# Attention and channel mixing of a transformer layer on one core: sums of the softmax weights in 32-column tiles spread by DMAs, one ring of score tiles, and fixed places for the side work

## The chip, the cores and the metric

The kernel runs on one core of a Trainium2 chip. A core has five engines that run their own instruction streams in order and wait for each other through semaphores: TensorE (PE in the profile; its weight loads are PEld), VectorE (DVE), ScalarE (ACT), GpSimd (POOL) and SyncE (SP), which here only issues DMAs. Matrix products are written to PSUM, eight banks of 512 fp32 columns in 128 partitions; everything else lives in SBUF. The metric is the device time of one execution in microseconds; lower is better. The kernel before takes 1331.07 us, the median of three runs from 1328.94 to 1338.77.

## The reference

Input x has 16 batches of 512 tokens with 128 channels. With xn the row-normalised x,

```python
xn = layernorm(x)                                   # (16, 512, 128)
# attention, 16 heads, key width 8, value width 64, causal
q, k, v = xn @ Wq, xn @ Wk, xn @ Wv
attn = softmax(where(causal, -inf, q k^T / sqrt(8)))
a = concat_heads(attn v) @ Wo
# channel mixing
xp = xn shifted down by one token, zeros first
xr, xk = mu_r*xn + (1-mu_r)*xp, mu_k*xn + (1-mu_k)*xp
f = sigmoid(xr @ W_r.T) * (relu(xk @ W_k.T)**2 @ W_v.T)
out = x + a + f
```

All of it is fp32.

## The kernel before, in words

The heads are taken in pairs, two pairs make a *group* (g, 0 to 3), and a batch has four groups. The causal blocks of a group (128 by 128 to 128 by 512) are packed into five *units* (`ROW_UNITS` for scores with rows in the partitions, `KEY_UNITS` for scores with keys in the partitions), so a batch has 20 units and the whole kernel 320. The program walks through *slots*, one for each unit (`slot_work(s)`, written out without loops on the chip). In slot s it does

- `row_scores` of unit s+8 (tile `sm`), of which VectorE takes the row maxima (`row_max`, tile `mx`); this finds the shift of the softmax ahead of time;
- `key_scores` of unit s (tile `sT`), with two extra rows of q that hold minus the row maximum in two parts, `weights` (Exp on ScalarE into tile `e`), the causal mask and the running sums `acc` on GpSimd;
- `weigh` of unit s-5, the product of the weights with v (tile `av`), and at the end of a pair `take_ctx`, which on VectorE multiplies `av` with the reciprocal sums (`recip`) into `ctx`. There is one `av` tile, so the next pair's first product waits for `take_ctx`.

Slots are named below by their number modulo 20 within a batch, and u is that number modulo 5. Around this come pieces of side work. `turn_stats` (once in a group) transposes the maxima on TensorE (`pm`), splits them on VectorE (`mh`, `ml`), and SP sends them with four DMAs into rows of q. `sum_weights` (twice in a group) sums weights over the keys with products by ones: tile `z`, 512 columns, two tiles of 64 array columns, one for each head; ScalarE makes the reciprocal by Ln and Exp(-x) into `recip`. `layernorm`, `transpose_xn`, `project_qk`, `spread_qk` and `project_v` prepare later batches: `spread_qk` is eight DMAs for q and eight for k in each batch, 128 KB each from DRAM into 8 partitions. `mix`, `ffn_r`, `ffn_k` and `ffn_out` are the channel mixing, `project_out` the product with Wo, `store` the result. The table built at the end of the kernel (`at(slot, ...)`) says in which slot each piece runs, always at the slot's end, ahead of `weigh`.

The engines are wrapped so that their instructions keep program order (`_InOrder`, line 57, which is why almost every profile line says L57); the order of the pieces is therefore written out by hand. Pools give tiles of one name a fixed number of buffers. PSUM is divided as follows: `ps_sm` three one-bank tiles, `ps_st` one two-bank tile, `ps_av` one bank, `ps_m` two banks (`m_tile`) that all side work shares: `xnTp`, `pq`, `pk`, `pv`, `pr`, `pkv`, `pm`, `z`, `po`, `yT`. `po` keeps one of the two for two slots, since `project_out` adds four pairs in it. All transfers of the steady state are issued by SP, in program order. In the built program they take eight completion semaphores in turn, and a transfer is issued only when the one before it on its semaphore, the eighth transfer back, has landed.

Of the kernel before, what the change touches and what calls it, by code (L numbers as in the profile page):

```python
# [15 lines left out]
P = 128  # L16
# [6 lines left out]
UNITS = 5  # L23
# [39 lines left out]
def attn_ffn_kernel(  # L63
# [26 lines left out]
    ctxp = ctx.enter_context(tc.tile_pool(name="ctxp", bufs=6))  # L90
# [4 lines left out]
    ps_sm = ctx.enter_context(tc.tile_pool(name="ps_sm", bufs=3, space=PSUM))  # L95
    ps_st = ctx.enter_context(tc.tile_pool(name="ps_st", bufs=1, space=PSUM))
    ps_av = ctx.enter_context(tc.tile_pool(name="ps_av", bufs=1, space=PSUM))
    ps_m = ctx.enter_context(tc.tile_pool(name="ps_m", bufs=2, space=PSUM))
# [94 lines left out]
    def layernorm(b):  # L193
        xt, st = xs[b], xs.pop((b, "st"))
        mv = small.tile([P, NB, 2], FP, tag="mv", name=f"mv_{b}")
        for c in range(NB):
            dve.bn_aggr(mv[:, c, :], st[:, c, :])
        ve = small.tile([P, NB], FP, tag="ve", name=f"ve_{b}")
        dve.tensor_scalar(ve, mv[:, :, 1], EPS, None, ALU.add)
        rstd = small.tile([P, NB], FP, tag="rstd", name=f"rstd_{b}")  # L200
        pool.tensor_tensor(rstd, ve, neg_half, ALU.pow)
        xn = one.tile([P, NB, D], FP, tag="xn", name=f"xn_{b}")
        for c in range(NB):
            dve.tensor_scalar(
                xn[:, c, :], xt[:, c, :], mv[:, c, 0:1], rstd[:, c : c + 1],
                ALU.subtract, ALU.mult,
            )
        xs[b, "n"] = xn
# [41 lines left out]
    def mix_prev(b, i):  # L250
        prev = one.tile([P, T], FP, tag="prev", name=f"prev_{b}_{i}")
        act.activation(prev, xnTs[b][:, 0:T], AF.Copy, scale=omm[:, i : i + 1])
        xmix[b, "prev"] = prev

    def mix(b, i):
        prev = xmix.pop((b, "prev"))
        xm = one.tile([P, T], FP, tag=f"xmix{i}", name=f"xmix_{b}_{i}")
        dve.scalar_tensor_tensor(
            xm, xnTs[b][:, 1 : T + 1], mus[:, i : i + 1], prev, ALU.mult, ALU.add
        )  # L260
        xmix[b, i] = xm


    def ffn_r(b):
        pr = m_tile(f"pr_{b}")
        product(pr, ffn_w[:, 0, :], xmix.pop((b, 0)))
        e = one.tile([P, T], FP, tag="e_sig", name=f"e_sig_{b}")
        act.activation(e, pr, AF.Abs)
        act.activation(e, e, AF.Exp, scale=-1.0)
        act.activation(e, e, AF.Ln, bias=1.0)  # L270
        s = one.tile([P, T], FP, tag="sig", name=f"sig_{b}")
        dve.scalar_tensor_tensor(s, pr, 0.0, e, ALU.min, ALU.subtract)
        ffns[b] = s

    def ffn_sig(b):
        act.activation(ffns[b], ffns[b], AF.Exp)
# [9 lines left out]
    def ffn_out(b):  # L286
        pk = m_tile(f"pkv_{b}")
        product(pk, ffn_w[:, 2, :], ffns.pop((b, "k")))
        f = one.tile([P, T], FP, tag="ffn", name=f"ffn_{b}")
        dve.tensor_tensor(f, pk, ffns[b], ALU.mult)  # L290
        ffns[b] = f
# [5 lines left out]
    def row_scores(n):  # L297
        b, g, u = place(n)
        q, k = qs[b % 2], ks[b % 2]
        for h in range(2):  # L300
            sms[n, h] = ps_sm.tile([P, 512], FP, tag="sm", name=f"sm_{n}_{h}")
        for pair, i, at_col in ROW_UNITS[u]:
            p = 2 * g + pair
            for h in range(2):
                s = slice(64 * h, 64 * h + RS)
                pe.matmul(
                    sms[n, h][:, at_col : at_col + (i + 1) * P],
                    q[s, p, i * P : (i + 1) * P], k[s, p, : (i + 1) * P],
                    start=True, stop=True,
                )  # L310

    def row_max(n, h):
        b, g, u = place(n)
        if u == 0 and h == 0:
            stats[b, g] = stat.tile([P, 2, 2, NB], FP, tag="mx", name=f"mx_{b}_{g}")
        sm = sms.pop((n, h))
        for pair, i, at_col in ROW_UNITS[u]:
            w = (i + 1) * P
            dve.tensor_tensor_reduce(
                out=sm[:, at_col : at_col + w], in0=sm[:, at_col : at_col + w],  # L320
                in1=row_mask[:, T - w : T],
                scale=1.0, scalar=LOWEST, op0=ALU.add, op1=ALU.max,
                accum_out=stats[b, g][:, h, pair, i : i + 1],
            )
# [89 lines left out]
    def sum_weights(q0, pair):  # L414

        e0, acc = es[q0 + 4 * pair], accs.pop((q0, pair))
        z = m_tile(f"z_{q0}_{pair}")
        for lo, hi, rhs in ((0, P, e0), (P, T, acc)):
            for h in range(2):
# [38 lines left out]
    def project_out(b, p):  # L458
        half = NPAIR // 2
        if p % half == 0:  # L460
            ffns[b, "po"] = m_tile(f"po_{b}_{p}")
        po = ffns[b, "po"]
        product(
            po, wo[:, p, :], ctxs.pop((b, p)), start=(p % half == 0), stop=(p % half == half - 1)
        )
# [16 lines left out]

    todo = {}

    def at(slot, f, *args):
        todo.setdefault(max(slot, -LEAD), []).append((f, args))

    for b in range(-2, B):
        s0 = b * PER_BATCH
        if 1 <= b + 2 < B:  # L490
            n = b + 2
            for c in range(NB):
                at(s0 + 5 + c, row_moments, n, c)
            at(s0 + 10, layernorm, n)
            at(s0 + 15, transpose_xn, n)
            at(s0 + 17, project_qk, n, False)
            at(s0 + 21, spread_qk, n, False)
            at(s0 + 23, project_qk, n, True)
# [12 lines left out]
        at(s0 + 1, ffn_r, b)  # L511
        at(s0 + 2, ffn_sig, b)
        at(s0 + 3, ffn_k, b)
        at(s0 + 4, ffn_out, b)
        for p, slot in enumerate((16, 16, 18, 18, 26, 26, 28, 28)):
            at(s0 + slot, project_out, b, p)
        at(s0 + 30, store, b)

    def slot_work(s):
# [3 lines left out]
        av_u = av % UNITS if av is not None else None  # L523
# [40 lines left out]
    take_ctx(N_UNITS - UNITS, 1)  # L564
    for s in sorted(todo):
        for f, args in todo[s]:
            f(*args)
# [31 lines left out]
```

## Time and profile before

| | us |
|---|---|
| median of 3 runs | 1331.07 (1328.94 to 1338.77) |
| profiled execution | 1328.98 |
| its span, first to last instruction | 1327.2 |
| TensorE busy | 1151.1 (87%) |
| VectorE / GpSimd / ScalarE busy | 811.8 / 733.2 / 641.2 |
| mean granted TensorE clock | 0.886 |
| first and last key scores start | 64.8 and 1309.9 |

Busy time is the union of an engine's instructions. The granted clock is the share of full speed at which TensorE was allowed to run; a matmul takes twice as long at 0.50. Durations below are means or medians of one instruction in this execution, so sums are made against its 1328.98 us, which is 2.1 us under the median.

### The profile page before, as it was taken

The page shows a single profiled execution, that of the slowest core. Times are in us where ns is not written, and L with a number is a line of the kernel's source. Part 1 is how long each engine was busy: PE and PEld are TensorE (multiplying, and loading weights), DVE is VectorE, ACT ScalarE, POOL GpSimd, SP SyncE. Part 2 cuts the span into 40 slices and gives each one's busy share as a digit, 9 for nine tenths or more (in the row PEclk, how much of TensorE's full clock was granted, in tenths as well). Part 3 has the DMA queues.
Part 4 walks back from the last instruction along what each step waited for, and adds up shares of the span by engine and source line. Part 5 has one row for each costly group of instructions (what it writes and reads, how often), then busy time and mean ns, then how long its engine had stood idle before and what let it go on. Part 6 is the DMA issues. An engine that isn't in the chain of part 4 may idle for free.

```text
span 1327.2 us, 19813 instructions
## 1 busy us (share of the span) xinstructions
PE 1151.1 (87%) x6659; PEld 492.3 (37%) x6659; DVE 811.8 (61%) x2659; ACT 641.2 (48%) x865; POOL 733.2 (55%) x964
## 2 busy tenths in 40 slices
PE   1779898898989988898898989888898898989898
PEld 0234343333434333343333334333343333434333
DVE  1575766656667556766646766665766656665741
ACT  0255555345554445555445554544545445455633
POOL 2065655556555555655546655555655655565645
PEclk9588998889889889989879988988988988998979
DMA  4440413205033130412304032231412304032000
GB/s 126 74 74 18 73 25 59 55 23 75 18 70 45 32 66 18 87 27 56 59 18 81 17 76 39 38 61 33 76 22 47 68 25 74 9 72 35 2 10 9
DMA packets 51509, 62.70 MB, mean 47 GB/s; under 512 B 6528, under 2 KB 26624, under 8 KB 51408
## 3 DMA queue, kind: packets, MB, share of 16 engines
q1 hardware_dynamic: 48768, 59.79, 24.5%
q10 hardware_dynamic: 2192, 1.38, 0.4%
q8 instruction: 53, 0.87, 0.3%
q0 software_dynamic: 448, 0.26, 0.2%
q14 instruction: 48, 0.39, 0.1%
HBM read 39.13 MB, written 20.97 MB: 45 GB/s over the span
## 4 chain that ended last, share of the span: by engine, by line
PE 62%; DVE 16%; DMA 8%; ACT 5%; POOL 5%; issue 3%; SPq 1%; DVEq 0%; POOLq 0%; ACTq 0%
PE av L57 17%; PE po L57 11%; PE z L57 9%; PE sm L57 8%; PE pv L57 6%; DVE sm L57 6%; PE sT L57 5%; DMA k<-k 4%; DVE xn L57 3%; PE pq L57 2%; ACT e_sig L57 2%; DVE xmix L57 2%; POOL acc L57 2%; DVE ctx L57 2%; ACT recip L57 2%
## 5 line engine op out<-in xcount | busy, mean ns | idle before, releaser
L57 DVE CUSTOM_DVE_ANT_0 sm<-sm,row_mask 128x384 f32<-128x384 f32 (+3 forms) x1024 | 495.3, 507 | 252.2 <-PE sm L57 237.5
L57 ACT ACTIVATE e<-sT 128x1024 f32<-128x1024 f32 x320 | 326.9, 1022 | 445.4 <-PE sT L57 440.3
L57 POOL TENSOR_SCALAR_AFFINE_SELECT e<-e 128x256 f32<-128x256 f32 (+1 forms) x448 | 197.6, 455 | 516.8 <-ACT e L57 513.3
L57 PE MATMUL av<-e,v 128*64 128x384 f32 (+3 forms) x2048 | 380.8, 474 | 7.6 <-DVE ctx L57 7.1
L57 POOL TENSOR_TENSOR acc<-acc,e 128x256 f32<-128x256 f32 (+1 forms) x256 | 255.8, 999 | 15.4
L57 POOL TENSOR_TENSOR acc<-e,e 128x768 f32<-128x768 f32 (+2 forms) x192 | 251.3, 1309 | 0.0
L57 PEld LDWEIGHTS av<-e,v 128*64 128x64 f32 x2048 | 148.3, 148 | 256.3 <-issue 202.3
L57 PE MATMUL sm<-k,q 33*128 33x384 f32 (+3 forms) x1024 | 184.2, 402 | 35.6 <-DVE mx L57 20.7
L57 PEld LDWEIGHTS sm<-k,q 33*128 33x128 f32 x1024 | 94.2, 206 | 226.0 <-issue 154.1
L57 PE MATMUL sT<-q,k 35*128 35x384 f32 (+3 forms) x1024 | 150.3, 344 | 5.9 <-DMA q<-ml 5.2
L57 PE MATMUL po<-ctx,wo 128*64 128x512 f32 x512 | 153.3, 729 | 0.0
L57 DVE DVE_READ_ACCUMULATOR2_ANT mx<- 128x1 f32 x1024 | 144.5, 141 | 0.0
L57 PE MATMUL pv<-wv,xnT 128*64 128x512 f32 x512 | 142.6, 658 | 0.0
L57 ACT ACTIVATE recip<-z 128x512 f32<-128x512 f32 x128 | 76.4, 597 | 129.9 <-PE z L57 129.9
L57 PE MATMUL z<-acc,ones 128*64 128x384 f32 x512 | 123.1, 557 | 0.0
L57 PE MATMUL z<-e,ones 128*64 128x128 f32 x512 | 58.9, 307 | 63.5 <-DVE ml L57 55.7
L57 DVE TENSOR_TENSOR ctx<-av,recip 128x512 f32<-128x512 f32 x128 | 88.3, 689 | 41.4 <-PE av L57 31.6
L57 PEld LDWEIGHTS sT<-q,k 35*128 35x128 f32 x1024 | 102.4, 205 | 14.9 <-issue 6.5
L57 ACT ACTIVATE v<-pv 128x512 f32<-128x512 f32 x128 | 76.5, 598 | 35.9 <-PE pv L57 35.9
L57 ACT ACTIVATE recip<-recip 128x512 f32<-128x512 f32 x128 | 80.7, 631 | 4.0
L57 PEld LDWEIGHTS z<-e,ones 128*64 128x64 f32 x512 | 27.7, 139 | 90.8 <-POOL e L57 60.8
L57 PEld LDWEIGHTS po<-ctx,wo 128*64 128x64 f32 x512 | 36.0, 157 | 59.1 <-issue 53.4
(63 smaller groups left out, 619.6 us busy)
## 6 DMA issues: line engine op xcount, KB each, us to landing
q<-q SPq DMA_DIRECT2D x120, 128.0 KB
k<-k SPq DMA_DIRECT2D x120, 128.0 KB
x<-in_L_attn_x_dram SPq DMA_DIRECT2D x16, 256.0 KB
q<-qh SPq DMA_DIRECT2D x16, 256.0 KB
q<-ql SPq DMA_DIRECT2D x16, 256.0 KB
k<-kh SPq DMA_DIRECT2D x16, 256.0 KB
k<-kl SPq DMA_DIRECT2D x16, 256.0 KB
out_dram<-o SPq DMA_DIRECT2D x16, 256.0 KB
```

What stands on the lines that cost most here:

```text
L57: return self._tc.keep_in_program_order(f(*args, **kwargs))
```

## The change

- PSUM: `sm` and `sT` come from one pool `ps_sc` of three two-bank tiles; `ps_m` has one bank instead of two.
- `sum_weights`: four tiles of 32 array columns; columns 0 to 255 and 256 to 511 of a head go to different partitions, so that `z` has 256 columns. Ln and Exp run on 256 columns into `half`; eight DMAs of 32 partitions by 1 KB (32 KB each), issued by SP, copy `half` into the full `recip`.
- Places: each piece of side work has a slot and one of three places in it: 0 after the scores, 1 after `sum_weights`, 2 after `weigh`. `sum_weights` runs at u = 4 and u = 1, `turn_stats` at the start of the slots with u = 2. `take_ctx` runs at the end of slots with u = 1 and u = 4, the former after the last product of the first pair, which is moved one slot earlier.
- `spread_qk`: 16 DMAs of 64 KB for q and 16 for k in a batch, in slots 1 to 4.
- `layernorm`: two passes of VectorE over 512 columns instead of four over 128. `mix`: both products on ScalarE and the sum on GpSimd. `ffn_r`: ScalarE copies `pr` to SBUF first. `project_out`: one group at a time, four sums on VectorE for a batch instead of two.

```diff
-    ps_sm = ctx.enter_context(tc.tile_pool(name="ps_sm", bufs=3, space=PSUM))
-    ps_st = ctx.enter_context(tc.tile_pool(name="ps_st", bufs=1, space=PSUM))
+    ps_sc = ctx.enter_context(tc.tile_pool(name="ps_sc", bufs=3, space=PSUM))
     ps_av = ctx.enter_context(tc.tile_pool(name="ps_av", bufs=1, space=PSUM))
-    ps_m = ctx.enter_context(tc.tile_pool(name="ps_m", bufs=2, space=PSUM))
+    ps_m = ctx.enter_context(tc.tile_pool(name="ps_m", bufs=1, space=PSUM))
...
-        for c in range(NB):
-            dve.tensor_scalar(
-                xn[:, c, :], xt[:, c, :], mv[:, c, 0:1], rstd[:, c : c + 1],
-                ALU.subtract, ALU.mult,
-            )
+        shape = [P, NB, D]
+        dve.tensor_tensor(xn, xt, mv[:, :, 0:1].to_broadcast(shape), ALU.subtract)
+        dve.tensor_tensor(xn, xn, rstd.unsqueeze(2).to_broadcast(shape), ALU.mult)
...
-    def mix_prev(b, i):
+    def mix(b, i):
+        xm = one.tile([P, T], FP, tag=f"xmix{i}", name=f"xmix_{b}_{i}")
         prev = one.tile([P, T], FP, tag="prev", name=f"prev_{b}_{i}")
+        act.activation(xm, xnTs[b][:, 1 : T + 1], AF.Copy, scale=mus[:, i : i + 1])
         act.activation(prev, xnTs[b][:, 0:T], AF.Copy, scale=omm[:, i : i + 1])
-        xmix[b, "prev"] = prev
-
-    def mix(b, i):
-        prev = xmix.pop((b, "prev"))
-        xm = one.tile([P, T], FP, tag=f"xmix{i}", name=f"xmix_{b}_{i}")
-        dve.scalar_tensor_tensor(
-            xm, xnTs[b][:, 1 : T + 1], mus[:, i : i + 1], prev, ALU.mult, ALU.add
-        )
+        pool.tensor_tensor(xm, xm, prev, ALU.add)
...
     def ffn_r(b):
         pr = m_tile(f"pr_{b}")
         product(pr, ffn_w[:, 0, :], xmix.pop((b, 0)))
+        s = one.tile([P, T], FP, tag="sig", name=f"sig_{b}")
+        act.activation(s, pr, AF.Copy)
         e = one.tile([P, T], FP, tag="e_sig", name=f"e_sig_{b}")
-        act.activation(e, pr, AF.Abs)
+        act.activation(e, s, AF.Abs)
         act.activation(e, e, AF.Exp, scale=-1.0)
         act.activation(e, e, AF.Ln, bias=1.0)
-        s = one.tile([P, T], FP, tag="sig", name=f"sig_{b}")
-        dve.scalar_tensor_tensor(s, pr, 0.0, e, ALU.min, ALU.subtract)
+        dve.scalar_tensor_tensor(s, s, 0.0, e, ALU.min, ALU.subtract)
+        act.activation(s, s, AF.Exp)
         ffns[b] = s
-
-    def ffn_sig(b):
-        act.activation(ffns[b], ffns[b], AF.Exp)
...
+        sm = sms[n] = ps_sc.tile([P, 2, 512], FP, tag="sc", name=f"sm_{n}")
...
-        st = sts[n] = ps_st.tile([P, 2, 512], FP, tag="sT", name=f"sT_{n}")
+        st = sts[n] = ps_sc.tile([P, 2, 512], FP, tag="sc", name=f"sT_{n}")
...
         e0, acc = es[q0 + 4 * pair], accs.pop((q0, pair))
         z = m_tile(f"z_{q0}_{pair}")
-        for lo, hi, rhs in ((0, P, e0), (P, T, acc)):
-            for h in range(2):
-                pe.matmul(
-                    z[64 * h : 64 * h + 64, lo:hi], ones, rhs[:, h, lo:hi],
-                    start=True, stop=True, skip_group_check=True,
-                )
+        for part in range(2):
+            for c in range(2):
+                if part and c:
+                    continue
+                lo, hi = ((0, P), (256, T))[c] if part == 0 else (P, 256)
+                for h in range(2):
+                    r = 64 * h + 32 * c
+                    pe.matmul(
+                        z[r : r + 32, lo - 256 * c : hi - 256 * c], ones[:, 0:32],
+                        (acc if lo else e0)[:, h, lo:hi],
+                        start=True, stop=True, skip_group_check=True,
+                    )
+        half = small.tile([P, 256], FP, tag="half", name=f"half_{q0}_{pair}")
+        act.activation(half, z[:, 0:256], AF.Ln)
+        act.activation(half, half, AF.Exp, scale=-1.0)
         r = small.tile([P, T], FP, tag="recip", name=f"recip_{q0}_{pair}")
-        act.activation(r, z, AF.Ln)
-        act.activation(r, r, AF.Exp, scale=-1.0)
+        for h in range(2):
+            for c in range(2):
+                for to in range(2):
+                    sp.dma_start(
+                        out=r[64 * h + 32 * to : 64 * h + 32 * to + 32, 256 * c : 256 * c + 256],
+                        in_=half[64 * h + 32 * c : 64 * h + 32 * c + 32],
+                    )
         recips[q0, pair] = r
...
-    def project_out(b, p):
-        half = NPAIR // 2
-        if p % half == 0:
-            ffns[b, "po"] = m_tile(f"po_{b}_{p}")
-        po = ffns[b, "po"]
-        product(
-            po, wo[:, p, :], ctxs.pop((b, p)), start=(p % half == 0), stop=(p % half == half - 1)
-        )
-        if p % half == half - 1:
-            y = one.tile([P, T], FP, tag=f"y{p // half}", name=f"y_{b}_{p}")
-            dve.tensor_tensor(y, po, ffns[b], ALU.add)
-            ffns[b] = y
+    def project_out(b, g):
+        po = m_tile(f"po_{b}_{g}")
+        for i in range(2):
+            product(po, wo[:, 2 * g + i, :], ctxs.pop((b, 2 * g + i)), start=i == 0, stop=i == 1)
+        dve.tensor_tensor(ffns[b], po, ffns[b], ALU.add)
...
-                at(s0 + 5 + c, row_moments, n, c)
-            at(s0 + 10, layernorm, n)
-            at(s0 + 15, transpose_xn, n)
-            at(s0 + 17, project_qk, n, False)
-            at(s0 + 21, spread_qk, n, False)
-            at(s0 + 23, project_qk, n, True)
-            at(s0 + 25, spread_qk, n, True)
+                at(s0 + 5 + c, 0, row_moments, n, c)
+            at(s0 + 10, 0, layernorm, n)
+            at(s0 + 12, 2, transpose_xn, n)
+            at(s0 + 15, 1, project_qk, n, False)
+            at(s0 + 17, 2, project_qk, n, True)
+            for i in range(2):
+                at(s0 + 21 + i, 0, spread_qk, n, False, slice(4 * i, 4 * i + 4))
+                at(s0 + 23 + i, 0, spread_qk, n, True, slice(4 * i, 4 * i + 4))
         if 0 <= b + 1 < B:
-            for n, slot in enumerate((9, 11, 11, 13, 13, 14, 19, 21)):
-                at(s0 + slot if b >= 0 else n - LEAD, project_v, b + 1, n)
+            places = ((5, 1), (8, 1), (9, 2), (10, 1), (13, 1), (14, 2), (18, 1), (19, 2))
+            for n, (slot, where) in enumerate(places):
+                if b >= 0:
+                    at(s0 + slot, where, project_v, b + 1, n)
+                else:
+                    at(n - LEAD, 1, project_v, b + 1, n)
         if b < 0:
             continue
         if b + 3 < B:
-            at(s0 + 12, load_x, b + 3)
-        at(s0 - 2, mix_prev, b, 0)
-        at(s0 - 1, mix, b, 0)
-        at(s0, mix_prev, b, 1)
-        at(s0 + 1, mix, b, 1)
-        at(s0 + 1, ffn_r, b)
-        at(s0 + 2, ffn_sig, b)
-        at(s0 + 3, ffn_k, b)
-        at(s0 + 4, ffn_out, b)
-        for p, slot in enumerate((16, 16, 18, 18, 26, 26, 28, 28)):
-            at(s0 + slot, project_out, b, p)
-        at(s0 + 30, store, b)
+            at(s0 + 12, 0, load_x, b + 3)
+        at(s0 - 3, 0, mix, b, 0)
+        at(s0 - 1, 0, mix, b, 1)
+        at(s0, 1, ffn_r, b)
+        at(s0 + 2, 2, ffn_k, b)
+        at(s0 + 4, 2, ffn_out, b)
+        for g in range(NQ):
+            at(s0 + 5 * g + 10, 2, project_out, b, g)
+        at(s0 + 27, 2, store, b)
...
     def slot_work(s):
         rows = s + LEAD if s + LEAD < N_UNITS else None
         keys = s if 0 <= s < N_UNITS else None
         av = s - LAG if 0 <= s - LAG < N_UNITS else None
-        av_u = av % UNITS if av is not None else None
+        u = s % UNITS
+        turned = s + LEAD - UNITS
+        if turned >= 0 and turned % UNITS == 0 and turned < N_UNITS:
+            b, g, _ = place(turned)
+            turn_stats(b, g)
         if rows is not None:
             row_scores(rows)
         if keys is not None:
@@ -528,27 +540,23 @@
             weights(keys)
             mask_weights(keys)
             add_weights(keys)
-        if av is not None and av_u == 0 and av >= UNITS:
-            take_ctx(av - UNITS, 1)
         if rows is not None:
-            row_max(rows, 0)
-        if av_u == 2:
-            weigh(av, only=0)
-            take_ctx(av - 2, 0)
-        if rows is not None:
-            row_max(rows, 1)
-        if 0 <= s + LEAD - UNITS < N_UNITS and (s + LEAD) % UNITS == 0:
-            b, g, _ = place(s + LEAD - UNITS)
-            turn_stats(b, g)
-        done = s - UNITS - (0 if s % UNITS == 0 else 2)
-        if s % UNITS in (0, 2) and 0 <= done < N_UNITS:
-            sum_weights(done, 0 if s % UNITS == 0 else 1)
-        for f, args in todo.pop(s, ()):
-            f(*args)
-        if av_u == 2:
-            weigh(av, only=1)
-        elif av is not None:
-            weigh(av)
+            row_max(rows)
+        run(s, 0)
+
+        if u == 4 and 0 <= s - 4 < N_UNITS:
+            sum_weights(s - 4, 0)
+        if u == 1 and 0 <= s - 6 < N_UNITS:
+            sum_weights(s - 6, 1)
+        run(s, 1)
+        if av is not None:
+            weigh(av, only=1 if u == 2 else None)
+            if u == 1:
+                weigh(av + 1, only=0)
+                take_ctx(av - 1, 0)
+            if u == 4:
+                take_ctx(av - 4, 1)
+        run(s, 2)
```

More of the change, by code (lines that the diff above doesn't have):

```diff
@@ L89, in attn_ffn_kernel @@
     ep = ctx.enter_context(tc.tile_pool(name="ep", bufs=LAG + 2))
-    ctxp = ctx.enter_context(tc.tile_pool(name="ctxp", bufs=6))
+    ctxp = ctx.enter_context(tc.tile_pool(name="ctxp", bufs=4))
     one = ctx.enter_context(tc.tile_pool(name="one", bufs=1))
@@ L288, in ffn_out @@
         product(pk, ffn_w[:, 2, :], ffns.pop((b, "k")))
-        f = one.tile([P, T], FP, tag="ffn", name=f"ffn_{b}")
+        f = small.tile([P, T], FP, tag="ffn", name=f"ffn_{b}")
         dve.tensor_tensor(f, pk, ffns[b], ALU.mult)
@@ L299, in row_scores @@
         q, k = qs[b % 2], ks[b % 2]
-        for h in range(2):
-            sms[n, h] = ps_sm.tile([P, 512], FP, tag="sm", name=f"sm_{n}_{h}")
+        sm = sms[n] = ps_sc.tile([P, 2, 512], FP, tag="sc", name=f"sm_{n}")
         for pair, i, at_col in ROW_UNITS[u]:
@@ L306, in row_scores @@
                 pe.matmul(
-                    sms[n, h][:, at_col : at_col + (i + 1) * P],
+                    sm[:, h, at_col : at_col + (i + 1) * P],
                     q[s, p, i * P : (i + 1) * P], k[s, p, : (i + 1) * P],
@@ L310, in row_scores, with row_max @@
                 )
-    def row_max(n, h):
+    def row_max(n):
         b, g, u = place(n)
-        if u == 0 and h == 0:
+        if u == 0:
             stats[b, g] = stat.tile([P, 2, 2, NB], FP, tag="mx", name=f"mx_{b}_{g}")
[L316 to L323, printed above, removed]
-            )
+        sm = sms.pop(n)
+        for h in range(2):
+            for pair, i, at_col in ROW_UNITS[u]:
+                w = (i + 1) * P
+                dve.tensor_tensor_reduce(
+                    out=sm[:, h, at_col : at_col + w], in0=sm[:, h, at_col : at_col + w],
+                    in1=row_mask[:, T - w : T],
+                    scale=1.0, scalar=LOWEST, op0=ALU.add, op1=ALU.max,
+                    accum_out=stats[b, g][:, h, pair, i : i + 1],
+                )
     def turn_stats(b, g):
@@ L417, in sum_weights @@
         z = m_tile(f"z_{q0}_{pair}")
-        for lo, hi, rhs in ((0, P, e0), (P, T, acc)):
-            for h in range(2):
-                pe.matmul(
-                    z[64 * h : 64 * h + 64, lo:hi], ones, rhs[:, h, lo:hi],
-                    start=True, stop=True, skip_group_check=True,
-                )
-        r = small.tile([P, T], FP, tag="recip", name=f"recip_{q0}_{pair}")
-        act.activation(r, z, AF.Ln)
-        act.activation(r, r, AF.Exp, scale=-1.0)
+        for part in range(2):
[13 more added lines that the diff above has]
+        act.activation(half, half, AF.Exp, scale=-1.0)
+        r = small.tile([P, T], FP, tag="recip", name=f"recip_{q0}_{pair}")
+        for h in range(2):
+            for c in range(2):
[3 more added lines that the diff above has]
+                        in_=half[64 * h + 32 * c : 64 * h + 32 * c + 32],
+                    )
         recips[q0, pair] = r
@@ L454, in take_ctx @@
         ctxs[b, 2 * g + pair] = c
-    def project_out(b, p):
-        half = NPAIR // 2
-        if p % half == 0:
-            ffns[b, "po"] = m_tile(f"po_{b}_{p}")
-        po = ffns[b, "po"]
-        product(
-            po, wo[:, p, :], ctxs.pop((b, p)), start=(p % half == 0), stop=(p % half == half - 1)
-        )
-        if p % half == half - 1:
-            y = one.tile([P, T], FP, tag=f"y{p // half}", name=f"y_{b}_{p}")
-            dve.tensor_tensor(y, po, ffns[b], ALU.add)
-            ffns[b] = y
+    def project_out(b, g):
[3 more added lines that the diff above has]
+        dve.tensor_tensor(ffns[b], po, ffns[b], ALU.add)
     def store(b):
@@ L483, in attn_ffn_kernel, with at @@
     todo = {}
-    def at(slot, f, *args):
-        todo.setdefault(max(slot, -LEAD), []).append((f, args))
+    def at(slot, where, f, *args):
+        if slot < -LEAD:
+            slot, where = -LEAD, 0
+        todo.setdefault((slot, where), []).append((f, args))
     for b in range(-2, B):
@@ L505, in attn_ffn_kernel, with run @@
         if b + 3 < B:
-            at(s0 + 12, load_x, b + 3)
-        at(s0 - 2, mix_prev, b, 0)
-        at(s0 - 1, mix, b, 0)
-        at(s0, mix_prev, b, 1)
-        at(s0 + 1, mix, b, 1)
-        at(s0 + 1, ffn_r, b)
-        at(s0 + 2, ffn_sig, b)
-        at(s0 + 3, ffn_k, b)
-        at(s0 + 4, ffn_out, b)
-        for p, slot in enumerate((16, 16, 18, 18, 26, 26, 28, 28)):
-            at(s0 + slot, project_out, b, p)
-        at(s0 + 30, store, b)
+            at(s0 + 12, 0, load_x, b + 3)
[7 more added lines that the diff above has]
+        at(s0 + 27, 2, store, b)
+    def run(s, where):
+        for f, args in todo.pop((s, where), ()):
+            f(*args)
     def slot_work(s):
@@ L563, in attn_ffn_kernel @@
         slot_work(s)
[L564 to L567, printed above, removed]
+    for s, where in sorted(todo):
+        run(s, where)
 _INS = [
```

## The prediction

> **What bounds the kernel now.** First the page's busy times and clock row.
>
> ```profile
> PE 1151.1 (87%) x6659; PEld 492.3 (37%) x6659; DVE 811.8 (61%) x2659; ACT 641.2 (48%) x865; POOL 733.2 (55%) x964
> ...
> PEclk9588998889889889989879988988988988998979
> ```
>
> TensorE is busiest, but a busy TensorE may be a slow one: the last row falls below 9 in most places. So next TensorE's waits (time, number, longest).
>
> ```profile
> PE z L57 <- DVE ml L57: 55.7, 30, 1.9
> PE pkv L57 <- POOL kr L57: 30.0, 16, 2.7
> PE sm L57 <- DVE mx L57: 20.7, 16, 2.2
> ```
>
> 46 waits of about 1.86 us: 30 on `ml`, where `po` holds one of the two `m` buffers and `z` needs the one that `pm` still occupies, and 16 on `kr`. Third, short stretches around one of them (time, TensorE busy, weight loads, VectorE, ScalarE, GpSimd, granted clock, DMA share, GB/s).
>
> ```profile
> 680.50:684.00 3.50, 1.64 (x15) 0.92 (x15) 2.52 (x7) 1.02 (x1) 3.23 (x4) 1.00 0.00 0
> 684.00:687.50 3.50, 2.81 (x12) 0.94 (x13) 0.00 (x0) 1.23 (x2) 0.41 (x1) 0.50 0.02 5
> 687.50:691.00 3.50, 3.50 (x18) 1.67 (x16) 1.61 (x6) 0.95 (x2) 0.00 (x0) 0.50 0.28 107
> ```
>
> TensorE idles 1.86 us before 683.9 and then has 0.50 of its clock for over 7 us. The trace's clock record holds 44 half-speed stretches after the prologue, 270 us, 6.1 us each: about one per such wait, each worth up to 3 us. **Work at full clock**: I took, for every kind of matmul, the time from its start to the next start where nothing idled and the clock was full, times its count: av 321, z 130, pv 116, po 113, sT 112, sm 109, the rest 102, in sum 1003 us. 1003 + 176 idle leaves 148 of the span for the clock. In steady state a batch takes 79.9 us (its q transfers start at 135.5 in batch 1 and 1173.6 in batch 14).
>
> **The queue that the change leans on.** SP issues transfers in order, and one waits for the eighth before it. The prologue shows it: eight q and eight k transfers of 96 KB (start, duration).
>
> ```profile
> 33.34 2.74 SPq L57 DMA_DIRECT2D q<-q  x8
> 36.87 9.60 SPq L57 DMA_DIRECT2D k<-k  x8
> ```
>
> The q issues take 2.74 us, 0.34 each; the k issues take 9.60, 1.33 apart, each waiting for a q transfer to land:
>
> ```profile
> SPq L57 <- DMA q<-q: 8.1, 8, 1.1
> ```
>
> So 96 KB pass per 1.33 us, 0.89 for 64 KB; by the semaphore events the 128 KB spreads land 1.55 (q) and 1.89 us (k) apart, 0.78 and 0.95 for 64 KB. I take 0.86. Meanwhile half of the DMA engines' time is used, at some 75 GB/s:
>
> ```profile
> 697.00:711.00 14.00, 12.99 (x87) 5.55 (x85) 11.79 (x34) 11.02 (x17) 9.55 (x13) 1.00 0.53 74
> 775.00:788.00 13.00, 11.98 (x81) 5.11 (x79) 10.98 (x32) 10.13 (x15) 8.74 (x10) 1.00 0.50 79
> ```
>
> **The change, part by part.** Rows (last columns: busy, mean ns):
>
> ```profile
> L57 ACT ACTIVATE e<-sT 128x1024 f32<-128x1024 f32 x320 | 326.9, 1022 | 445.4 <-PE sT L57 440.3 <-POOL acc L57 5.1
> L57 PE MATMUL z<-acc,ones 128*64 128x384 f32 x512 | 123.1, 557 | 0.0
> L57 PE MATMUL z<-e,ones 128*64 128x128 f32 x512 | 58.9, 307 | 63.5 <-DVE ml L57 55.7 <-DVE sig L57 7.8
> L57 ACT ACTIVATE recip<-z 128x512 f32<-128x512 f32 x128 | 76.4, 597 | 129.9 <-PE z L57 129.9
> L57 DVE SCALAR_TENSOR_TENSOR xmix<-xnT,mus,prev 128x512 f32<-128x512 f32 x32 | 42.6, 1331 | 0.0
> L57 DVE TENSOR_SCALAR xn<-x,mv,rstd 128x128 f32<-128x128 f32 x64 | 41.7, 714 | 22.9 <-POOL rstd L57 21.8 <-POOL xnT L57 1.1
> ```
>
> *z.* 128 sums cost 130 us at full clock, 1.01 each. The two heads' 64-column matmuls start 7 ns apart, so side by side. With four tiles at once the longest is 256 columns instead of 512: 65 us saved. No row shows four; two at a time would save nothing. I take 65, as pairs already run so. Ln and Exp shrink from 0.597 + 0.631 to about 0.39 + 0.42 (slope between 512 and 1024 columns), 53 us of ScalarE.
>
> *Waits.* `z` no longer shares a slot with `pm` (u = 1 and 4 against 2), and `ffn_out` runs two slots after `ffn_k`: the 46 waits go. What is late next is below.
>
> *Moved work.* `mix` adds 32 x 0.71 us to ScalarE and 32 sums to GpSimd (`kr`: 1.04; `acc`, same width: up to 1.27), and takes 43 us off VectorE. `ffn_r`'s copy adds 10 us to ScalarE. `layernorm` has two passes per batch, at 0.69 (`ffn`) to 1.86 us (an `xn` pass beside a GpSimd sum); I take 0.9 (`xmix` alone). `po` adds 32 x 0.69. VectorE, ScalarE and GpSimd come to some 790, 620 and 770 us and bound nothing.
>
> *One `m` bank.* Each piece now waits for its predecessor's eviction. That hurts where VectorE is late: in slot 10 layernorm (about 3.5 us with the wait for `rstd`) stands ahead of the `po` sum, so `z` in slot 11 waits some 1.9 us; `pq` and `pk` wait for `lo` behind the maxima, 1.1 in sum. In the score ring, key scores need the previous slot's maxima done, 2.3 of some 3 us: covered.
>
> *The reciprocal's DMAs.* 1024 more on SP. Alone they hide: eight issues 2.7, landing about 2 (32 KB in the prologue: 2.2; 4 KB rows: 1.8), against over two slots until `take_ctx`. The prologue's 32 KB transfers were issued 0.34 apart and overlapped, so by that row their overhead costs latency alone. "DMA: Bandwidth & Descriptors" of the Trainium skill (Rules for kernel authors) speaks against the change here: under 64 KB a transfer is mostly overhead. Were that overhead paid eight times in turn, at the row's 2 us, a reciprocal would take an estimated 16 us, and pair 0 would be late in all 64 groups.
>
> But in slots 1 to 4 SP's order is: q first half, eight reciprocals, four `mh`/`ml`, q second half, k first half, k second half, eight reciprocals of slot 4. Each waits for its eighth predecessor. From the start of slot 19 (mod 20):
> 1. Slot 19's reciprocal is ready at 4.3: scores 0.95, Exp 1.02, mixing 2 x 0.71, Ln and Exp 0.8; first landing at 6.3, which lets the first q transfer go.
> 2. That lands 2.9 later (between 2.2 for 32 KB and 4.1 for 128 KB), the eighth 7 x 0.86 on: 15.2. Slot 1's last reciprocal is issued then, and four row transfers (0.64 each): 18.1.
> 3. q second half: 18.1 + 2.9 + 6.0 = 27.0; k, 16 x 0.86 later: 40.8. Only then does the last reciprocal of slot 4 go: + 1.9 landing + 0.7 `ctx` = **43.4**.
>
> `take_ctx` wants it at the end of slot 6. By its own work and waits TensorE is there, and through the scores of slot 7, at 29.5. Behind the waiting `ctx` on VectorE stand `mh`, `ml` and all maxima; the one `av` tile waits for it on TensorE. So TensorE idles some **13 us in each of 15 batches**. The last batch has no spread.
>
> From there to the next slot 19: full-clock work 12 x 1.69 (scores, av) + 4 z (2.0) + 3 pm (0.6) + 6 pv (5.5) + 2 po (3.5) + pq, pk (1.8) + two transposes (1.2), less 0.95 done, 33.9. Waits 4.1 (1.9 and 1.1 above, 1.1 while VectorE catches up). Clock: the long stall's half-speed stretch 2.5, the one behind layernorm 2.4 (6.1 us long, half lost, 8 of 10 times). **Batch: 43.4 + 33.9 + 4.1 + 4.9 = 86.3 us against 79.9.**
>
> On the clock, "TensorE: Matmul & The Clock Gate" (HAM oscillation — how this bites in real kernels) states no TensorE idle gap over about 3.4 us as the rule. Here 1.86 us was enough 46 times for 44 stretches, so the row decides. By the rule the gap behind layernorm would be free, 2.4 less in each of 14 batches, 34 us.
>
> **Sum**, against the profiled 1329 us (the median is 2 higher): batch 0 +11 (its chain ends at 99.9, where before is at 89), 14 x 6.4 = +90, last batch and tail -12 (no stall, z halved, waits gone): **1418 us, 6.7% slower.**
>
> **Rivals.**
> - *The queue does not hold the reciprocals* (they land before `take_ctx`): 1003 - 65 = 938, prologue 50, other waits 16 x 5, clock 38: about 1110. For it: waits and clock losses truly go. Against: the 1.33 us lock step. 6%.
> - *Faster, by the same stall but clean slots.* Every batch needs chain plus the rest under 79.9; with chain and work at 77.3, it decides when waits, clock and transfer pace together add less than 2.6 us instead of 9. At q's pace for all (0.78: -2.6) and 3 us of waits and clock, 77.7 a batch: 1293. For it: before, layernorm cost 1.3. Against: a 13 us idle surely halves the clock. 13% for 1293 to 1342, half of it within 1%.
> - *Heavier:* k's pace for all (0.95: +2.9), z two at a time (+2), waits and clock 13: 95 a batch, 1543. 8% above 1480.
> - *The change does not do what it says:* TensorE waits move into `ctx` instead of going. That is my forecast.
>
> **How the numbers follow.** 73% for 1342 to 1480, likeliest 1418. The range 1300 to 1500 leaves about 1 in 8 out and reaches to the clean-slot case and most of the heavy one. This kernel's measurement tells about 1% from no change. Faster by over 1%: 6 + 6 = 12%; within: 7%; slower: 81%.
>
> **What would show it.** Right: TensorE's `av` waits on `ctx`, 15 times some 12 us; VectorE's `ctx` waits on transfers into `recip`; SP waits on k transfers; `z` on `ml` and `pkv` on `kr` gone; TensorE busy under 1100; z's union near half. Wrong: reciprocals of slot 4 landing within 6 us of their Exp, or the stall under 6 us.

## The result, and the profile after

The changed kernel takes **1440.0 us** (median of 4 runs, 1437.1 to 1444.0) against 1333.1 us for the kernel before on the same chip: 1.080 times as long, interval 1.075 to 1.085. The forecast was 1418 us, 1300 to 1500. The profiled execution spans 1442.3 us. Ratios here and below leave out executions in a slower state, of which only the last kernel below had any (2 of 10). Busy times and clock row of its page:

```profile
PE 1081.2 (75%) x7171; PEld 462.3 (32%) x7171; DVE 801.8 (56%) x2627; ACT 615.8 (43%) x913; POOL 762.2 (53%) x996
...
PEclk9969979798897988989799797979979798797999
```

TensorE is busy 70 us less than before, in a span 115 us longer. I overlaid its busy stretches with the clock record and split the busy time into what full clock would have needed and what low clock added:

| us | before | after |
|---|---|---|
| TensorE busy, as if at full clock | 1011 | 999 |
| added by a low clock while busy | 140 | 83 |
| idle between its first and last matmul | 161 | 346 |

So the clock gave back 57 us and the work itself little (the clock's record leaves some 25 us open between the first two rows; what the sums save is measured below); 185 us of new idle time took more than both. TensorE's waits name it (time, number, longest):

```profile
PE av L57 <- DVE ctx L57: 198.2, 19, 16.3
PE sT L57 <- DMA q<-ml: 33.4, 42, 2.4
PE z L57 <- DVE ffn L57: 31.8, 62, 0.9
PE pv L57 <- DVE kl L57: 20.3, 15, 1.4
```

The 46 waits on `ml` and `kr` are gone. (`q<-ml` stands for the transfers of the row maxima into q, called row transfers below.) In their place the weighted sum waits 198 us for a context: 15 of these waits are longer than 2.5 us, one in each batch but one, 8.1 to 16.3 us, 13.1 on average. The contexts wait on VectorE for the reciprocals' transfers, and SP's queue meanwhile waits for spread transfers to land, 356 times:

```profile
DVE ctx L57 <- DMA recip<-half: 221.8, 22, 17.1
```

```profile
SPq L57 <- DMA k<-k: 87.4, 193, 0.9
...
SPq L57 <- DMA q<-q: 79.1, 163, 1.0
```

One whole burst on SP's queue (start, duration of the issues, count):

```profile
672.36 4.99 SPq L57 DMA_DIRECT2D recip<-half  x8
677.45 2.88 SPq L57 DMA_DIRECT2D q<-q  x8
680.55 6.77 SPq L57 DMA_DIRECT2D recip<-half  x8
687.42 1.39 SPq L57 DMA_DIRECT2D q<-mh  x2
688.90 1.29 SPq L57 DMA_DIRECT2D q<-ml  x2
690.29 2.84 SPq L57 DMA_DIRECT2D q<-q  x8
693.23 12.36 SPq L57 DMA_DIRECT2D k<-k  x16
```

The sixteen k issues take 12.36 us although an unhindered issue takes 0.35 (the second row: 2.88 for eight). The reciprocal of slot 4 comes only after them, from 706.61 on. By the semaphore events the k issue of 693.23 lands at 699.62, and only then does the issue of 699.63 go, eight transfers later; that one lands at 706.53, and the first copy of slot 4's reciprocal goes at 706.61. The last copy is issued at 711.26 and has landed at 713.14. VectorE and TensorE at that moment (start, duration, and in brackets how long each stood before, and for what):

```profile
713.55 0.69 DVE L57 TENSOR_TENSOR ctx<-av,recip 128x512 f32<-128x512 f32 x1 [14.01 <-DMA recip<-half]
```

```profile
714.30 1.12 PE L57 MATMUL av<-e,v 128*64 128x256 f32 x4 [13.25 <-DVE ctx L57]
```

And the clock around it (time, TensorE busy, weight loads, VectorE, ScalarE, GpSimd, granted clock, DMA share, GB/s):

```profile
695.00:702.00 7.00, 5.83 (x47) 2.58 (x43) 2.26 (x6) 2.57 (x4) 2.92 (x4) 0.98 0.54 82
702.00:714.30 12.30, 0.00 (x1) 0.01 (x1) 0.75 (x2) 0.17 (x1) 2.21 (x3) 0.64 0.38 81
714.30:721.00 6.70, 6.70 (x28) 3.29 (x28) 4.78 (x17) 1.62 (x2) 2.00 (x3) 0.50 0.15 38
721.00:728.00 7.00, 7.00 (x46) 2.69 (x44) 4.99 (x23) 3.89 (x6) 3.47 (x5) 0.89 0.18 52
```

TensorE stands, and then works at half its clock, for 8.3 us by the clock's record (until 722.6).

The rows that the prediction priced (last columns: busy, mean ns):

```profile
L57 PE MATMUL z<-acc,ones 128*32 128x256 f32 x512 | 81.3, 396 | 0.9 <-POOL acc L57 0.9
L57 ACT ACTIVATE half<-half 128x256 f32<-128x256 f32 x128 | 53.4, 417 | 4.1
L57 ACT ACTIVATE half<-z 128x256 f32<-128x256 f32 x128 | 48.3, 377 | 13.4 <-PE z L57 7.2 <-DMA recip<-half 6.1
L57 POOL TENSOR_TENSOR xmix<-xmix,prev 128x512 f32<-128x512 f32 x32 | 40.9, 1278 | 26.6 <-ACT prev L57 26.6
L57 DVE TENSOR_TENSOR xn<-xn,rstd 128x512 f32<-128x512 f32 x16 | 11.1, 692 | 14.6 <-POOL rstd L57 13.7 <-POOL xnT L57 0.9
```

### The profile page after: what moved, and what is told of

Read it like the earlier page. It is cut to its first block, busy times and chain, and to the rows that moved or that the text cites. A ratio compares the mean times of both kernels' runs of the same rounds, so it can differ in the third digit from the quotient of the medians.

```text
span 1442.3 us, 22978 instructions
## 1 busy us (share of the span) xinstructions
PE 1081.2 (75%) x7171; PEld 462.3 (32%) x7171; DVE 801.8 (56%) x2627; ACT 615.8 (43%) x913; POOL 762.2 (53%) x996
## 4 chain that ended last, share of the span: by engine, by line
PE 37%; DMA 28%; DVE 14%; SPq 8%; ACT 7%; issue 3%; POOL 2%; DVEq 0%; ACTq 0%
DMA k<-k 13%; PE av L57 11%; DMA q<-q 8%; SPq L57 8%; PE pv L57 7%; DVE sm L57 5%; PE sm L57 5%; DMA recip<-half 3%; PE po L57 3%; PE sT L57 3%; PE z L57 3%; DMA q<-ml 2%; DVE ctx L57 2%; DVE ffn L57 2%; POOL rstd L57 2%
## 5 line engine op out<-in xcount | busy, mean ns | idle before, releaser
L57 DVE CUSTOM_DVE_ANT_0 sm<-sm,row_mask 128x384 f32<-128x384 f32 (+3 forms) x1024 | 507.8, 498 | 140.8 <-PE sm L57 114.6
L57 PE MATMUL av<-e,v 128*64 128x384 f32 (+3 forms) x2048 | 368.1, 472 | 198.2 <-DVE ctx L57 198.2
L57 POOL TENSOR_TENSOR acc<-acc,e 128x256 f32<-128x256 f32 (+1 forms) x256 | 256.1, 1000 | 15.4
L57 PEld LDWEIGHTS av<-e,v 128*64 128x64 f32 x2048 | 132.3, 144 | 364.2 <-DVE ctx L57 203.1
L57 PE MATMUL pv<-wv,xnT 128*64 128x512 f32 x512 | 164.5, 726 | 38.4 <-DVE kl L57 20.3
L57 PE MATMUL po<-ctx,wo 128*64 128x512 f32 x512 | 130.0, 629 | 10.4 <-DVE ql L57 7.9
L57 DVE TENSOR_TENSOR ffn<-po,ffn 128x512 f32<-128x512 f32 x64 | 44.0, 687 | 112.4 <-PE po L57 112.4
L57 PE MATMUL z<-acc,ones 128*32 128x256 f32 (+1 forms) x1024 | 81.3, 335 | 0.9 <-POOL acc L57 0.9
L57 PE MATMUL z<-e,ones 128*32 128x128 f32 x512 | 53.8, 286 | 31.8 <-DVE ffn L57 31.8
L57 PEld LDWEIGHTS pv<-wv,xnT 128*64 128x64 f32 x512 | 28.1, 150 | 95.9 <-ACT half L57 52.4
L57 ACT ACTIVATE half<-half 128x256 f32<-128x256 f32 x128 | 53.4, 417 | 4.1
```

The lines of the kernel that those rows point to most:

```text
L57: return self._tc.keep_in_program_order(f(*args, **kwargs))
```

## The experiments

**The theory**: the stall needs two things on one in-order queue, the burst of 32 spread transfers that land one after another, and the reciprocal's copies, which must pass behind it. Either alone is harmless. **The rivals**: the copies alone are too late, or too dear to issue, whatever the burst does; or the burst alone does it.

Four kernels ran together first (kernel before: 1329.2 us).

**Old sums.** The kernel after, with the sums of the kernel before and no copies:

```diff
-        for part in range(2): ...            # four 32-column tiles, half, eight copies
+        for lo, hi, rhs in ((0, P, e0), (P, T, acc)):
+            for h in range(2):
+                pe.matmul(z[64 * h : 64 * h + 64, lo:hi], ones, rhs[:, h, lo:hi], ...)
+        act.activation(r, z, AF.Ln)
+        act.activation(r, r, AF.Exp, scale=-1.0)
```

> The kernel after with the sums of before: two 64-column tiles, 512 columns, Ln and Exp at full width, no copies of the reciprocal; all else as after. Queue theory (SP's in-order queue holds slot 4's reciprocal behind the spread of q and k): the 198 us of TensorE waits of av on ctx go, some 37 us of half clock behind them too, the waits on the maximum's transfers (33 us) mostly; z costs 49 us more TensorE work: about 1225 us (1195 to 1260). Rival (one m bank, one score ring and the new places cost the time, the copies lie beside): stalls stay, over 1400 us. Rival (the copies are slow wherever they stand): as the queue theory, about 1225.

Measured: **1206.3 us**, ratio 0.906 (0.899 to 0.913), inside the range. TensorE's waits:

```profile
PE z L57 <- DVE ffn L57: 26.4, 63, 0.9
PE sT L57 <- DMA q<-ml: 23.3, 9, 4.1
...
PE av L57 <- DVE ctx L57: 3.5, 6, 0.9
```

The stall is gone; the burst still holds a few row transfers back (9 waits of up to 4.1 us). That the bank, the ring or the places cost the time is out with it. All other parts of the change together make this kernel 9.4% faster than before; the new sums turned that into a loss.

**Spread sent apart** (the spread-out kernel below). The kernel after, its copies kept, but two spread transfers per slot over sixteen slots, behind the slot's other work:

```diff
-                at(s0 + 21 + i, 0, spread_qk, n, False, slice(4 * i, 4 * i + 4))
-                at(s0 + 23 + i, 0, spread_qk, n, True, slice(4 * i, 4 * i + 4))
+                for j in range(4):   # one of the four places, both heads
+                    at(s0 + 20 + 8 * i + j, 2, spread_qk, n, False, slice(4 * i, 4 * i + 4), j)
+                    at(s0 + 24 + 8 * i + j, 2, spread_qk, n, True, slice(4 * i, 4 * i + 4), j)
```

> The kernel after with the 32 spread transfers of a batch at two per slot over 16 slots, behind the slot's sums, instead of 32 in slots 1 to 4; the copies of the reciprocal stay. Queue theory: at most two or four spread transfers stand ahead of a reciprocal, so the stalls go: about 1190 us (1160 to 1230), av's waits on ctx under 30 us. Rival (m bank, ring and places): unchanged, about 1440. Rival (the copies are slow wherever they stand): over 1380, with the waits of ctx on the copies spread over all 64 groups.

Measured: **1255.4 us**, ratio 0.942 (0.934 to 0.951).

```profile
PE sT L57 <- DMA q<-ml: 59.0, 67, 2.5
...
PE av L57 <- DVE ctx L57: 8.7, 16, 1.1
```

With the same 1024 copies the stall is gone (8.7 us in all), so the copies alone do not make it. (The edit also moves the spread from ahead of a slot's copies to behind them; the next kernel leaves it where it was.) But the time lies above the range, and what is late next is plain: the score matmuls wait 67 times for the row transfers. SP's queue shows what stands ahead of them:

```profile
705.52 4.95 SPq L57 DMA_DIRECT2D recip<-half  x8
710.51 0.83 SPq L57 DMA_DIRECT2D q<-q  x2
711.44 1.39 SPq L57 DMA_DIRECT2D q<-mh  x2
712.93 1.29 SPq L57 DMA_DIRECT2D q<-ml  x2
```

Eight copies keep SP for 4.95 us with nothing late ahead of them, 0.63 each, and the rows of the maxima stand behind them.

**Half of the burst.** The kernel after without the spread of pairs 4 to 7 from batch 2 on (those pairs then compute with an older batch's q and k):

```diff
-            for i in range(2):
+            for i in range(2 if n < 2 else 1):
```

> The kernel after without the second halves of the spread (pairs 4 to 7 of q and k stay as they were two batches earlier) for batches 2 to 15: 16 transfers in a batch instead of 32, in slots 1 and 3. Queue theory: the chain to slot 4's reciprocal is shorter by some 12 us (two groups of eight transfers at 0.7 us each), the stall falls from 13 to 0 to 2 us in 14 of 15 batches: about 1230 us (1200 to 1265). A dose between: if half the transfers remove clearly less than 9 us a batch, the queue is not all of it. Other rivals: about 1440.

Measured: **1267.0 us**, ratio 0.952 (0.944 to 0.959), just above the range. Waits:

```profile
PE sT L57 <- DMA q<-ml: 35.7, 36, 3.0
PE av L57 <- DVE ctx L57: 35.2, 17, 5.0
```

The wait for contexts falls from 198 to 35 us, and five waits are left above 2.5 us, the longest 5.0: the stall follows the length of the burst.

**The new sums alone.** The kernel before, at its own places, with the new sums:

```diff
+        (sum_weights of the kernel after: four tiles, half, eight copies)
-    ctxp = ctx.enter_context(tc.tile_pool(name="ctxp", bufs=6))
+    ctxp = ctx.enter_context(tc.tile_pool(name="ctxp", bufs=5))
```

> The kernel before with the new sums alone: four 32-column tiles, 256 columns and eight copies of the reciprocal by SP; order, banks and places of before (five instead of six ctx buffers, for room). Queue theory: the eight q transfers of 128 KB in slot 1 stand ahead of slot 2's row maxima and reciprocal, which come some 8 us late once a batch; z saves 49 us: 1400 us (1360 to 1440), slower than before. Rival (the copies are harmless, the new places and banks cost the time): about 1285, faster than before. Rival (the copies are slow wherever they stand): over 1400, late in all 64 groups.

Measured: **1644.8 us**, ratio 1.236 (1.226 to 1.246): the direction as expected, the size far off. By its time it goes to the rival that the copies are slow wherever they stand. TensorE's waits, and one of SP's queue:

```profile
PE av L57 <- DVE ctx L57: 154.7, 81, 4.5
PE sT L57 <- DMA q<-ml: 149.1, 26, 9.5
PE z L57 <- DVE ml L57: 55.6, 30, 3.8
```

```profile
SPq L57 <- DVE ml L57: 229.0, 36, 12.3
```

I had priced the burst and not the groups without one. Here 81 contexts are late, where the kernel after has 19, and score matmuls wait up to 9.5 us for row transfers; the granted clock falls to 0.80. On VectorE 49 contexts wait for copies, in 48 of the 64 groups (that rival had all 64), and 46 of them belong to second pairs. In the order of before, the copies of a second pair are issued behind the row transfers, and SP waits 229 us for the `ml` that these carry. So something in the rest of the change makes the copies bearable in most groups of the kernel after. It may be this order on the queue, or the places, from which a first pair's sum has more time until its context (slot 4 to the end of slot 6 of its group, against slot 5 to the middle of slot 7). That is argued, not shown: the 316 us were not taken apart.

What was open after this: whether the price that is left in the spread-out kernel is the order on the queue or the time of the copies. Four more kernels ran together (kernel before: 1327.7 us).

**Old sums, spread apart**: both edits above at once.

> The kernel after with the old sums (as in the run that undid them, 1206 us, 9.3% below before) and with its spread sent two transfers per slot over sixteen slots. If the 23 us of waits of the score matmuls for the row transfers (9 waits of up to 4.1 us) come from the spread's burst on the queue, they go: 1180 us (1168 to 1195), that is 11% below before, with under 8 us of that wait left. The rival: the row transfers are late for another reason, or meet the spread in more groups: 1206 within 8 us, the wait as it was.

Measured: **1179.4 us**, ratio 0.888 (0.885 to 0.891), inside the range; the wait for row transfers is gone from the list. Without copies, the burst itself costs 27 us.

**Rows ahead of copies**, on the spread-out kernel:

```diff
+            copy_out(q0, 0)                   # in sum_weights, pair 0 as before
...
             turn_stats(b, g)
+        if u == 2 and 0 <= s - 7 < N_UNITS:
+            copy_out(s - 7, 1)                # pair 1: one slot later, behind the rows
```

> The spread-out kernel (1255 us) with the copies of the second pair's reciprocal issued one slot later, behind the four row transfers and not ahead of them. If what is left over is the row transfers standing behind 5 us of copies on SP's queue, the 59 us of score waits for them fall below 15 and the clock rises with them: 1205 us (1190 to 1225). The rival: the copies are then late for the context multiplication, VectorE stands, and the waits of the weighted sum (8.7 us) take the place: 1250 or more.

Measured: **1349.9 us**, ratio 1.017 (1.014 to 1.020): outside the range, and the rival's way. Waits, and SP's queue in one group:

```profile
PE av L57 <- DVE ctx L57: 62.1, 39, 5.7
PE pv L57 <- DVE ffn L57: 53.4, 14, 4.5
```

```profile
709.20 1.51 SPq L57 DMA_DIRECT2D q<-q  x4
713.79 1.40 SPq L57 DMA_DIRECT2D q<-mh  x2
715.29 1.29 SPq L57 DMA_DIRECT2D q<-ml  x2
716.68 5.12 SPq L57 DMA_DIRECT2D recip<-half  x8
```

The row transfers leave the wait of the scores, but SP stands from 710.7 to 713.8 until VectorE has made `mh`; the copies now queue behind that wait, and contexts come late (39 waits, up to 5.7 us), with `ffn` behind them on VectorE. The order on the queue only chooses who is late.

**Half as many copies**, on the spread-out kernel: the exponential writes four pieces to where they belong, and only the other four are copied.

```diff
-        act.activation(half, half, AF.Exp, scale=-1.0)
...
-        for h in range(2): for c in range(2): for to in range(2): (eight copies)
+        for c in range(2):
+            for h in range(2):
+                own, to = 64 * h + 32 * c, 64 * h + 32 - 32 * c
+                cols = slice(256 * c, 256 * c + 256)
+                act.activation(r[own : own + 32, cols], half[own : own + 32], AF.Exp, scale=-1.0)
+                sp.dma_start(out=r[to : to + 32, cols], in_=r[own : own + 32, cols])
```

> The spread-out kernel (1255 us) with the exponential written in four pieces to its own place and only the other four of the eight copies issued. If SP's 0.63 us for each copy is the price, each pair's issue falls from 5.0 to 2.5 us and the score waits for the row transfers from 59 to some 20 us: 1220 us (1200 to 1238). The rival: three more ScalarE instructions of some 0.3 us for each pair (an estimate from 0.42 us for 256 elements), 120 us on ScalarE in all, make the waits for ScalarE dearer (16.7 us now): 1255 or more.

Measured: **1166.0 us**, ratio 0.878 (0.876 to 0.881): better than its range, the best of all, 12% below the kernel before and 19% below the kernel after. No score matmul waits for a row transfer any more, and contexts cost TensorE 3.7 us. ScalarE's groups of this kernel:

```profile
L57 ACT ACTIVATE recip<-half 32x256 f32<-32x256 f32 x512 | 212.3, 415 | 13.3
...
L57 ACT ACTIVATE half<-z 128x256 f32<-128x256 f32 x128 | 48.3, 377 | 4.7 <-PE z L57 4.6
```

A quarter of the partitions takes as long as all of them (415 ns against 417), so ScalarE works 159 us more. It is busy 772 of 1165 us; `pr`, `pv` and `pq` of TensorE now wait 28 us in all for its copies `v`, the only new price of any size that the waits show.

**Both**, half as many copies and rows ahead:

> Both: four copies for each pair, and those of the second pair behind the row transfers. If the queue is all that is left, the rest should be that of the kernel with old sums and spread out, less the 49 us of TensorE work that the new sums save (130 to 81): 1150 us (1130 to 1180). If the clock or ScalarE takes the saving back, no better than the old sums spread out.

Measured: **1189.3 us**, ratio 0.896 (0.893 to 0.899), above the range, no better than the old sums spread apart (the rival's mark), and 23 us slower than half copies alone. Half copies alone keep the saving, so it is the order that costs here too; that it costs less because fewer copies wait behind the rows is likely, not shown.

That the copies' issue time is a price was shown for the spread-out kernel. The last run asked how much of the stall in the burst it is.

**Half as many copies, burst kept**: the same edit on the kernel after itself.

> The kernel after, its burst of thirty-two spread transfers left where it is, with only four of the eight copies of each reciprocal issued (the exponential writes the other four places itself). If the copies' 0.63 us of issue are what makes the queue late, the three pairs in the way of the stalled context lose 3 x 2.5 = 7.5 us, so the stall of each batch falls from 13.1 to some 5.6 us, most of the 33 us of score waits for the row transfers goes, and some 2 us of half clock with them: 1440 - 15 x 11.6 = 1265 us (1235 to 1300). The rival: the burst itself, whose transfers land 0.53 to 0.7 us apart whatever stands between them, holds the copies back; then the stall stays above 10 us: 1390 or more.

Measured: **1350.7 us** (kernel before: 1329.1), ratio 1.013 (1.009 to 1.017), between the two. The wait for the rows is gone, as expected; the stall is not, which is the rival's mark. TensorE's waits, and SP's queue in one burst:

```profile
PE av L57 <- DVE ctx L57: 157.3, 21, 14.9
```

```profile
717.29 2.85 SPq L57 DMA_DIRECT2D q<-q  x8
720.24 12.81 SPq L57 DMA_DIRECT2D k<-k  x16
733.66 6.37 SPq L57 DMA_DIRECT2D recip<-recip  x8
```

The stalls (14 above 2.5 us) average 10.9 us instead of 13.1. The k issues take as long as in the kernel after, and the copies still go when they end: from the first q issue to the last landing the burst takes 31.7 us on average, against 32.9. Copies with half the issue time hardly hurry it, so in the burst it is the pace of landings that holds: over the 14 bursts of this run the stall and the burst's length correlate by 0.999. Three gains can be read in the 89 us between the two kernels. The waits for contexts fall by 41 us (each stall is 2.2 us shorter, and one is gone), the row waits by 33, and the low clock's share by 15 (82.6 to 67.2). Some 27 us of new waits for ScalarE's `v` stand against them, so this is not an exact account.

The burst and the number of copies in one table (us):

| copies for each reciprocal | burst of 32 | spread apart |
|---|---|---|
| none (old sums) | 1206 | 1179 |
| four | 1351 | 1166 |
| eight | 1440 (the change) | 1255 |

Down the last column: eight copies cost 76 us more than they save, four save 13. The burst costs 27 us without copies and 185 us with either number of them: it is the two together. The theory stands, but neither alone was harmless, and the copies' issue time is a second, smaller price; of the rivals, "the copies alone" explains 76 us of the 234 that the new sums cost.

## Why the prediction was right, point by point

**The chain** is the one that was written down, step for step. From the start of slot 19 (668.50 in the burst shown), predicted and seen:

| step, us from the start of slot 19 | predicted | seen |
|---|---|---|
| slot 19's reciprocal ready, first copy issued | 4.3 | 3.9 |
| first q transfer issued | 6.3 | 9.0 |
| q first half landed | 15.2 | 18.3 |
| q second half begins | 18.1 | 21.8 |
| k landed | 40.8 | 41.2 |
| slot 4's context done | 43.4 | 45.7 |
| TensorE at its wait | 29.5 | 32.6 |
| stall | some 13 | 13.25 |

Batches are 86.6 us apart (15 stalls, 105.3 to 1317.5), predicted 86.3. Within the chain two sizes were off, and nearly cancel:
- *Eight issues 2.7* (0.34 for each copy): a copy takes SP 0.63 us, so eight take 5.0. That moves the first q transfer by 2.6 us and slot 4's last landing by some 2.
- *0.86 us for 64 KB*: over 14 bursts the q transfers land 0.79 and the k transfers 0.76 us apart. The stall goes with the burst's length: the shortest of the 14 (27.8 us from the first q issue to the last landing) has a stall of 10.4 us, the longest (36.1) one of 15.4, and over all the two correlate by 0.79.

**Rest of the batch**: 42.4 us from the context of this stall to the next slot 19, predicted 42.9; its terms were less good than their sum. On average over the batches the rest is 41.6 us and the chain 45.1, so that the batch came out within 0.3 us is partly luck.
- *z, 65 us saved*: mis-sized. The two kernels with spread apart and hardly any low clock (old sums, and new sums with half the copies) differ in TensorE's busy time by what the sums save:

```profile
PE 1037.8 (88%) x6659; PEld 457.0 (39%) x6659; DVE 800.7 (68%) x2627; ACT 678.0 (58%) x913; POOL 764.6 (65%) x996
```

```profile
PE 998.8 (86%) x7171; PEld 430.4 (37%) x7171; DVE 795.1 (68%) x2627; ACT 772.0 (66%) x1297; POOL 761.5 (65%) x996
```

  39 us, not 65. One sum takes 0.57 us from its start to the next matmul's (669.17 to 669.74), where I had taken half of 1.01. And 1.01 was too much for the old sum: that is its time in the kernel before where a transpose follows it, and where `av` follows it takes 0.91 there and 0.89 in the first of these two kernels. From 0.89 to 0.57, 128 times, is 41 us.
- *1.9 us behind layernorm, and 2.4 of clock*: the two `xn` passes take 0.68 and 0.69, not 0.9, and `z` waits at most 0.9 us for `ffn`. A low clock seldom follows gaps of that length (below).
- *Not foreseen*: 33 us of score matmuls waiting for row transfers, 42 times. I had queued the copies before those transfers and given the transfers 0.64 us each, but had not asked who waits for the rows. Eight of the nine such waits of 1.5 us and more (one is the 1.82 us before 690.79) are followed by a low clock, 0.78 on average from 688 to 695.
- *pq and pk wait 1.1*: moved. `pv` waits 1.4 us once a batch, for `kl`.

**The clock rule.** Counted in the kernel after by the clock's record: idle gaps of TensorE of 0.5 to 1.0 us are followed by a low clock in 2 of 56 cases, of 1.0 to 1.5 us in 4 of 34, of 1.5 to 2.6 us in 9 of 10, and of 8 us and more in 15 of 15. So here too some 1.5 us was mostly enough, and the 3.4 us that "TensorE: Matmul & The Clock Gate" (HAM oscillation — how this bites in real kernels) of the Trainium skill gives as the bound is too wide for this kernel. In the kernel before I had counted too neatly: of its 46 waits 35 are followed by one of the 44 stretches, and six of the other nine stretches begin after waits of 1.3 us for the maxima. After the prologue, all stretches of both kernels but the last of each, which the end cuts short, last 3.41 us or a multiple of it, up to 10.2 before and 20.5 after.

**The transfer rule.** "DMA: Bandwidth & Descriptors" (Rules for kernel authors) of the Trainium skill has transfers under 64 KB as mostly overhead; the prediction let it make every group late by landings in turn. In the trace the eight copies from 672.36 on, with nothing ahead of them, land 1.8 us after issue, each while the next are under way: the overhead is not paid in turn as landing. But 0.63 us of issue is paid in turn, and halving it was worth 89 us (1255 against 1166). The rule pointed the right way, against the change, by another route than the one that I weighed; but size alone does not set this price, as a 64 KB spread transfer is issued in 0.35.

**The sum.** 1418 was 24 us short of the span. The first stall ends at 105.3 instead of 99.9 (+5), the batches add 4, and from the last stall to the end it is 124.8 us instead of 109.9 (+15): there too the scores wait for row transfers (6.2 us) and `po` for a late context (2.5 us), and the clock drops three times, to 0.88 from 1380 to 1400 and to 0.86 from 1420 on.

**The rivals.** *The queue does not hold* is out: it holds. *Clean slots* needed under 2.6 us of waits, clock and pace together for each batch; the row waits alone are 2.2 and the clock 5.5 (83 us in 15 batches). *Heavier* was no nearer: `z` was slower than half, but the transfers ran nearer to q's pace. That pace and k's, which told these two rivals apart, had been read in one batch (1.55 and 1.89 us for 128 KB); over 14 batches of the kernel before they average 1.87 and 1.82, so there were no two paces to choose between. That the waits move into the context, which I called my forecast, is what the waits show.

## What to carry to other kernels

A small transfer put on a queue like this one, which starts its transfers in order and each only when the eighth before it has landed, inherits the landing time of the bulk that stands ahead of it. Before a short latency is priced, therefore, write down the queue's order over the whole period in which the bulk passes. Send bulk in small parts between the short ones: it cost 185 us not to. Then count what each issue keeps the queue for and who stands behind it; here fewer copies, paid for with work on an engine that had room, gave more than any order of them.

## What the runs showed of the hardware that I had not expected

- A copy of 32 partitions by 256 elements (32 KB) kept SP's queue 0.63 us, a spread transfer of 64 KB on 8 partitions 0.35. The smaller transfer was the dearer one to issue.
- An exponential of 256 elements took 415 ns on 32 partitions and 417 ns on 128.
- The same 64 KB transfers landed 0.56 to 0.94 us apart (means over the eight q transfers of a half or the sixteen k transfers of a burst) in one execution, with the same instructions in every batch; what sets the pace of a burst was not found.
